# PSUM rings written out by hand, an earlier copy out of the attention bank, and a reordered start in a four-layer fp32 network

## The chip, the cores and the metric

The kernel runs on one core of one Trainium2 chip, all in fp32. The metric is the device time of one execution in microseconds (us), as the median of some runs. One further execution was profiled, and its own time differs a little from that median.

The core has five engines with their own instruction queues: TensorE (PE, with its weight loads, PEld), VectorE (DVE), ScalarE (ACT), GpSimd (POOL) and SyncE (SP), which here only issues DMAs. ScalarE's and GpSimd's queues issue DMAs too. Matmuls write into PSUM, which has eight banks of 128 partitions x 512 fp32 numbers; VectorE and ScalarE read it.

## The reference

The input is x with 4 images of 512 channels and 32 x 32 = 1024 tokens. Each layer adds its result to x after a group norm (32 groups of 16 channels):

```python
x = x + L0(gn(x))   # attention with mixed heads
x = x + L1(gn(x))   # gate per channel
x = x + L2(gn(x))   # plain attention
x = x + L3(gn(x))   # memory of 2048 rows, best 8 per token
```

- Layer 0: q, k and v are 512 x 512 projections, in 8 heads of 64. The scores of the heads are mixed by an 8 x 8 matrix, put through a softmax over the keys, and normalized over the whole map of each head (instance norm, with gamma and beta). They then weigh v; a projection with a bias follows.
- Layer 1: the mean of each channel goes through a small circuit of rotations, whose angles are q_params, and through a linear map with a sigmoid. This gives one factor for each channel.
- Layer 2: softmax attention in 8 heads with projections of q, k, v and of the result.
- Layer 3: each token is multiplied with 2048 memory rows; the softmax of the 8 largest products weighs these 8 rows.

## The kernel before, in words

**Tiling.** B = 4 images, KC = 4 blocks of 128 channels, T = 1024 tokens, TC = 8 blocks of 128 tokens, NB = 512 columns. The layers are not run one after the other over all images: layer 0 goes through the four images; what belongs to layer 1 and the preparation of the next image are pieces laid between its steps; then layers 2 and 3 follow. Most instructions carry `pin`, which keeps them in program order on their engine, so the order of the code is the order of the queues. Instructions without it are placed by a scheduler.

**PSUM in layer 0.** Three double banks (`pairs`, L52) and two single ones, `pv_bank` (L53) and `pt_bank` (L54), are allocated once. Projections take `pairs[at % 3]` by an index given by the caller (`place`, L176). Small results go to `pt_bank`.

**The start.** Nine small parameters are loaded by ScalarE's queue (L64 to L82), among them b_proj, while SyncE's queue loads x's four blocks of channels and w_q, block by block (`first`, L299 to L303). GpSimd makes an identity (L87) and the averaging matrix of the groups, `gavg` (L93). For each block k, `stats(k)` (L308) takes statistics on VectorE, `means(k)` averages them over each group with a matmul, and has the deviations formed by three small GpSimd operations (L150 to L152). `deviations(k)` averages again and takes a power on GpSimd (L119), `normalize(k)` scales the block on VectorE (L326). `multiply(k, m)` adds block k's share to the q projection (L332). The order is written out at L338 to L354. Then `circuit` (L772) prepares layer 1's tables: it reads w_head in 32 tiny loads (L781), and its chain of VectorE operations is ahead of the evacuation of k (L414).

**A step of layer 0.** An image has STEPS = 32 steps of 32 queries. Each computes scores (L467), copies them out (ScalarE, L473), brings them into another layout by 8 DMAs, which SyncE and GpSimd issue (L482), mixes heads (L493), takes exps (ScalarE, L500), turns them (VectorE, L506) and gathers statistics (L521). Seven steps behind (LAG = 7), `apply` (L523) weighs v with them and adds up in `pv_bank`, over four steps for each tile j. `take_out(b, j)` (L590) then has ScalarE copy `pv_bank` into a tile with the tag o1, which GpSimd scales (L605). Seven further steps, 32 to 38, end the image (L1559). In steps 32 to 35 the next image's q projections run as `piece` (L1510), one in each, into `pairs[(s + 1) % 3]`, and `put_q` (L291) has ScalarE copy q out. In `step` (L1436) `take_out` comes after `piece`: in step 34, tile j = 6 is copied behind that step's q. After the last image q belongs to layer 2 and is evacuated by VectorE (L1145).

**From layer 0 to layer 2.** Behind the last image come k (indices m + 1, L1569), v (i + 2, L1586) and the output projection `put_out` (m, L1588; evacuated on VectorE at L684, statistics at L699). Then the PSUM pool is closed and two new pools are opened: `ps_s` with three double banks and `ps_m` with two single ones (L1590 to L1595). In layers 2 and 3 each product takes a new tile from these pools.

**Layers 2 and 3.** `scores2` (L1165) computes four score tiles of a unit (L1183); ScalarE takes their exps (L1177). `apply2` (L1206) weighs v with the unit before (L1220). `invert2` (L1240) takes another tile for the sums of the softmax (`rs`, L1251). `seven` (L1033) computes a projection from seven products of half-size blocks; in `seven_k` ScalarE copies the first of them out four times (L1073). `attention` (L1326) multiplies with the memory, `read` and `read_last` (L1400, L1387) put together and transpose the result.

Of the kernel before, what the change touches and what calls it, by code (L numbers as in the profile page):

```python
# [10 lines left out]
F32 = mybir.dt.float32  # L11
# [30 lines left out]
def fast_net(ctx: ExitStack, tc: tile.TileContext, a: dict, out: bass.AP, flag: bass.AP):  # L42
# [18 lines left out]
        return pt_bank  # L61


    def chan(src, name):  # L64
        t = const.tile([P, KC], F32, tag=name, name=name)
        nc.scalar.dma_start(out=t, in_=src)
        return t

    gamma = const.tile([P, NH], F32, tag="gamma", name="gamma")
    nc.scalar.dma_start(out=gamma, in_=a["in_gamma"].partition_broadcast(P))  # L70
    beta = const.tile([P, NH], F32, tag="beta", name="beta")
    nc.scalar.dma_start(out=beta, in_=a["in_beta"].partition_broadcast(P))
    bproj = chan(a["b_proj"], "bproj")
    bq2 = chan(a["bq"], "bq2")
    bk2 = chan(a["bk"], "bk2")
    bp2 = chan(a["bp"], "bp2")
    fcb = chan(a["fc_b"], "fcb")

    fcw = const.tile([NQ, C], F32, tag="fcw", name="fcw")
    nc.scalar.dma_start(out=fcw, in_=a["fc_w"])  # L80
    qpar = const.tile([P, NL * NQ], F32, tag="qpar", name="qpar")
    nc.scalar.dma_start(out=qpar, in_=a["q_params"].partition_broadcast(P))  # L82

    whp = const.tile([P, NH], F32, tag="whp", name="whp")

    ident = const.tile([P, P], F32, tag="ident", name="ident")
    make_identity(nc, ident)  # L87
    ones = const.tile([P, P], F32, tag="ones", name="ones")
    nc.gpsimd.memset(ones, 1.0)
    mhalf = const.tile([P, NH], F32, tag="mhalf", name="mhalf")  # L90
    nc.gpsimd.memset(mhalf, -0.5)

# [8 lines left out]
        out=gavg_v, in_=gavg_v, compare_op=ALU.is_ge, fill=0.0, base=GSZ - 1,  # L101
        pattern=[[GSZ, P // GSZ], [0, GSZ]], channel_multiplier=-1,
    )
    NS = 32


# [68 lines left out]

    def place(at, name):  # L176

        return pairs[at % 3] if at is not None else ps_s.tile([P, 2, NB], F32, tag="sc", name=name)

    def flat2(ps):  # L180
        return ps.rearrange("p n q -> p (n q)")
# [112 lines left out]
    def first():  # L294

        I = img[0]
        xn = I["xn"] = xn_all
        w = I["w_q"] = eight_k([P, KC, C], "w_q0_0", 0)
        for k in range(KC):  # L299
            nc.sync.dma_start(out=xn[:, k, :], in_=x_v[0, :, k, :])  # L300
            nc.sync.dma_start(out=w[:, k, :], in_=a["w_q"][:, k, :])
        I["w_k"] = load_w("w_k", "w_k0_0", 1)
        I["w_v"] = load_w("w_v", "w_v0_0", 2)  # L303
        q = I["q"] = big("q", "q0_0")
        ybar = I["ybar"] = small.tile([P, KC], F32, tag="ybar", name="ybar0")
        parts, found = {}, {}

        def stats(k):  # L308
            mv = small.tile([P, 2], F32, tag="mv0", name=f"mv0_{k}")
            st = small.tile([P, 2, 6], F32, tag="bnst", name=f"st_a0_{k}")  # L310
            for i in range(2):
                pin(nc.vector.bn_stats(st[:, i, :], xn[:, k, i * NB:(i + 1) * NB]))
            pin(nc.vector.bn_aggr(mv, st.rearrange("p i s -> p (i s)")))
            parts[k] = group_coeffs_parts(mv[:, 0:1], mv[:, 1:2], f"a0_{k}")

        def means(k):
            next(parts[k])
            next(parts[k])

        def deviations(k):  # L320
            next(parts[k])
            found[k] = next(parts[k])

        def normalize(k):
            gm, rstd, dm = found[k]
            pin(nc.vector.tensor_scalar(  # L326
                xn[:, k, :], xn[:, k, :], gm, rstd, ALU.subtract, ALU.mult))
            pin(nc.gpsimd.tensor_mul(ybar[:, k:k + 1], dm, rstd))

        def multiply(k, m):  # L330
            for n in range(T // NB):
                pin(nc.tensor.matmul(  # L332
                    pairs[m][:, n, :],
                    w[:, k, m * P:(m + 1) * P], xn[:, k, n * NB:(n + 1) * NB],
                    start=(k == 0), stop=(k == KC - 1),
                ))
# [696 lines left out]
    def seven(b, key, src, multiply, view, block, begin, done=None):  # L1033

        a11, s2, s5, a22 = quarters(img[b][key], H)
        s1, s6, s7 = places7[key]
        b11, t6, t7, b22 = quarters(src, NB)
        t1, t3, t4 = places7["in"]
        factors = {1: (s1, t1), 2: (s2, b11), 3: (a11, t3), 4: (a22, t4),
                   5: (s5, b22), 6: (s6, t6), 7: (s7, t7)}  # L1040
        for i, (at, uses) in enumerate(SEVEN):
            ps = ps_s.tile([P, 2, NB], F32, tag="sc", name=f"{key}_{b}_{at}")
# [122 lines left out]
    def scores2(b, u, before=None):  # L1165
# [12 lines left out]
            es.append(e)  # L1178

        for i, t in enumerate(range(t0, t0 + 4)):  # L1180
            sc = ps_s.tile([P, 2, NB], F32, tag="sc", name=f"sc_{nm}_{t}")
            for r in range(2):
                pin(nc.tensor.matmul(  # L1183
                    sc[:, r, :],
                    I["k"][r * HD:(r + 1) * HD, m, t * P:(t + 1) * P],
                    I["q"][r * HD:(r + 1) * HD, m, n * NB:(n + 1) * NB],
                    start=True, stop=True,
                ))
            scs.append(sc)
            if before is None or i < 2:  # L1190
                exp2()
# [14 lines left out]
    def apply2(b, u, exp2=None):  # L1206
# [33 lines left out]
    def invert2(b):  # L1240
# [4 lines left out]
            return  # L1245
        m, n = I["ready"] = due
        nm = f"{b}_{m}_{n}"
        ps = ps_s.tile([P, 2, NB], F32, tag="sc", name=f"rs_{nm}")[:, 0, 0:NS]
# [77 lines left out]
    def attention(b, tt, between=None):  # L1326
# [2 lines left out]
        att = eight_k([P, NI], f"att_{nm}")  # L1329
        for i, (lo, hi) in enumerate(  # L1330
                ((0, T), (T, T + NB), (T + NB, NI)) if (b, tt) == tiles[-1] else ((0, T), (T, NI))):
            sc = ps_s.tile([P, T], F32, tag="sc", name=f"at_{nm}_{i}")
# [54 lines left out]
    def read_last(b, tt, picked, dg):  # L1387

        got, et, rs, xr = picked
        tp = ps_m.tile([P, KC, P], F32, tag="mm", name=f"stp_{b}_{tt}")  # L1390
        for i in range(TOPK):
            for m in range(KC):
                pin(nc.tensor.matmul(
# [6 lines left out]
    def read(b, tt, picked):  # L1400
# [9 lines left out]
        tp = ps_m.tile([P, KC, P], F32, tag="mm", name=f"stp_{nm}")  # L1410
# [25 lines left out]
    def step(b, s, mid, piece):  # L1436
# [103 lines left out]
    for b in range(B):  # L1540
# [38 lines left out]
        if last:  # L1579
# [13 lines left out]
    stage = ctx.enter_context(ExitStack())  # L1593
    ps_s = stage.enter_context(tc.tile_pool(name="ps_s2", bufs=3, space=PSUM))
    ps_m = stage.enter_context(tc.tile_pool(name="ps_m2", bufs=2, space=PSUM))  # L1595

    def small_ps(name):
        return ps_s.tile([P, 2 * NB], F32, tag="sc", name=name)
# [81 lines left out]
    def check_range():  # L1680

        tot = small.tile([P, 1], F32, tag="tot", name="tot")
        nc.vector.tensor_reduce(tot, seen0, AX.X, ALU.add)
        tps = ps_m.tile([P, NB], F32, tag="mm", name="tot")
# [748 lines left out]
```

## Time and profile before

| | before |
|---|---|
| median of 3 runs | 2556.93 us (2554.43 to 2558.5) |
| the profiled execution, its own time | 2558.39 us |
| span from its first to its last instruction | 2556.6 us |
| mean granted clock of TensorE | 0.998 |
| layer 0, four images with layer 1 between | about 0 to 1267 us of the span |
| layer 2 | about 1267 to 2090 us |
| layer 3 | to the end |
| matmuls in the span | 18534 instructions |

The profile gives the busy time of each engine and its share of the span. It lists what ended each idle time of an engine, as "waited for", and shows timelines of single engines. Each row of a timeline holds the start, the length, the engine, the line of the code, the operation, and the tile written from the tile read; equal neighbours are merged (x16). In brackets is the idle time ahead of it with what ended it. The fp32 matmuls of the program are two instructions each in the trace, each with its own weight load.

### The profile page before, as it was taken

What the parts mean: (1) busy time and instruction counts of PE and PEld (TensorE: products, weight loads), DVE (VectorE), ACT (ScalarE), POOL (GpSimd) and SP (SyncE); (2) the same over time, 40 slices, a digit from 0 to 9 for tenths busy, and PEclk for the clock granted to TensorE, in tenths of its full rate; (3) what the DMA queues carried; (4) which work ended last, traced back from release to release, by engine and by line L of the source; (5) the groups of instructions that cost most, each with busy time, mean ns of one, the idle gap of its engine ahead of it and who ended that gap; (6) DMA issues with size and microseconds to landing.
All of it is one profiled execution on the core that took longest, in us unless ns stands there. A gap on an engine that the chain in (4) does not pass through costs nothing.

```text
span 2556.6 us, 47828 instructions
## 1 busy us (share of the span) xinstructions
PE 2503.3 (98%) x18534; PEld 1180.8 (46%) x18534; DVE 1685.8 (66%) x2785; ACT 985.8 (39%) x1177; POOL 1192.5 (47%) x1700
## 2 busy tenths in 40 slices
PE   8999999999999999999999999999999999999998
PEld 3344534554355534555633533453353344444445
DVE  4599448872688438881267567576657648788875
ACT  1467336651666336651153145125314612121211
POOL 3266415553465425553074147117405617566655
PEclk9999999999999999999999999999999999999999
DMA  2578438872698428982301130121014046767665
GB/s 83 145 207 237 125 120 226 244 211 74 172 243 235 131 82 211 244 248 101 124 16 55 70 112 18 54 83 59 21 54 148 18 130 190 219 186 217 187 184 170
DMA packets 187211, 361.39 MB, mean 141 GB/s; under 512 B 32729, under 2 KB 96217, under 8 KB 182882
## 3 DMA queue, kind: packets, MB, share of 16 engines
q1 hardware_dynamic: 105744, 178.71, 22.6%
q0 software_dynamic: 49152, 142.79, 20.6%
q10 hardware_dynamic: 32082, 36.76, 5.3%
q8 instruction: 149, 2.44, 0.4%
q14 instruction: 84, 0.69, 0.1%
HBM read 186.96 MB, written 36.96 MB: 88 GB/s over the span
## 4 chain that ended last, share of the span: by engine, by line
PE 74%; issue 10%; POOL 7%; DVE 3%; ACT 3%; DMA 2%; POOLq 0%; SPq 0%; ACTq 0%; DVEq 0%
PE pair L192 10%; PE sc_c L1183 9%; PE pv_c L1220 9%; PE pv L532 8%; POOL got L1360 7%; PE pair L467 6%; PE pair L493 5%; PE pt L425 5%; PE pt L721 4%; PE q L192 3%; PE Wk L1056 3%; PE Wv L1063 3%; ACT e L500 2%; PE Wp L1056 2%; PE at L1335 2%
## 5 line engine op out<-in xcount | busy, mean ns | idle before, releaser
L482 POOL DMA_DIRECT2D s<-ss x512 | 258.2, 511 | 399.5 <-PE pair L493 113.4
L506 DVE STREAM_TRANSPOSE eT<-e 128x1024 f32<-128x1024 f32 x256 | 316.5, 1236 | 193.6 <-ACT e L500 193.0
L1360 POOL DMA_INDIRECT got<-in_mem,ix x256 | 279.5, 1092 | 213.2 <-issue 122.1
L1177 ACT ACTIVATE eT<-sc_c 128x1024 f32<-128x1024 f32 x256 | 248.0, 1022 | 330.7 <-PE sc_c L1183 204.8
L521 DVE BATCH_NORM_STATS2 st<-e 128x6 f32<-128x256 f32 x1024 | 350.7, 404 | 0.0
L500 ACT ACTIVATE e<-pair 128x1024 f32<-128x1024 f32 x256 | 250.7, 1022 | 167.5 <-PE pair L493 137.2
L1201 POOL TENSOR_TENSOR e<-eT 128x1024 f32<-128x1024 f32 x96 | 232.3, 2421 | 168.6 <-DVE out L1125 69.5
L467 PE MATMUL pair<-k,q 64*32 64x512 f32 x4096 | 267.4, 598 | 12.7 <-ACT e L500 12.7
L473 ACT COPY ss<-pair 128x1024 f32<-128x1024 f32 x256 | 247.3, 1020 | 77.5 <-DMA s<-ss 37.9
L532 PE MATMUL pv<-eT,v 128*64 128x128 f32 x4096 | 250.7, 276 | 8.9 <-ACT pv L592 8.9
L532 PEld LDWEIGHTS pv<-eT,v 128*64 128x64 f32 x4096 | 221.1, 137 | 76.7 <-issue 54.5
L1183 PE MATMUL sc_c<-q,k 64*128 64x512 f32 x1024 | 240.9, 607 | 3.1 <-DVE xr L684 2.3
L1220 PE MATMUL pv_c<-eT,v 128*64 128x512 f32 x1024 | 233.0, 597 | 0.0
L1202 DVE TENSOR_TENSOR eT<-eT,e 128x1024 f32<-128x1024 f32 x96 | 136.3, 1420 | 146.3 <-POOL e L1201 146.1
L1197 POOL TENSOR_TENSOR eT<-eT 128x1024 f32<-128x1024 f32 x32 | 77.8, 2433 | 206.8 <-ACT eT L1177 202.8
L1407 DVE SCALAR_TENSOR_TENSOR acc<-got,et,acc 128x512 f32<-128x512 f32 x210 | 157.9, 752 | 7.5
L493 PE MATMUL pair<-s,wmix 32*32 32x512 f32 x4096 | 160.6, 600 | 2.3 <-issue 2.1
L1183 PEld LDWEIGHTS sc_c<-q,k 64*128 64x128 f32 x1024 | 93.6, 187 | 141.0 <-issue 71.9
L1340 ACT COPY att<-at 128x1024 f32<-128x1024 f32 (+1 forms) x65 | 64.9, 999 | 219.7 <-PE at L1335 212.9
L467 PEld LDWEIGHTS pair<-k,q 64*32 64x32 f32 x4096 | 57.0, 105 | 179.9 <-ACT e L500 86.2
L1220 PEld LDWEIGHTS pv_c<-eT,v 128*64 128x64 f32 x1024 | 68.0, 137 | 136.8 <-issue 136.8
L1335 PE MATMUL at<-memT,xn_d 128*128 128x512 f32 x256 | 120.7, 594 | 0.0
(335 smaller groups left out, 3431.3 us busy)
## 6 DMA issues: line engine op xcount, KB each, us to landing
s<-ss SPq DMA_DIRECT2D x512, 128.0 KB
s<-ss POOLq DMA_DIRECT2D x512, 128.0 KB
rb<-r POOLq DMA_DIRECT2D x64, 128.0 KB
o<-o SPq DMA_DIRECT2D x32, 256.0 KB
xr<-in_x ACTq DMA_DIRECT2D x32, 256.0 KB
x<-xr SPq DMA_DIRECT2D x32, 256.0 KB
xr_c<-x SPq DMA_DIRECT2D x32, 256.0 KB
rb_c<-r SPq DMA_DIRECT2D x64, 128.0 KB
```

The lines of the kernel that those rows point to most:

```text
L192: pin(nc.tensor.matmul(ps[:, n, :], w[:, k, m * P:(m + 1) * P], rhs(k, n), start=(k == 0), stop=(k == KC - 1),))
L467: pin(nc.tensor.matmul(sc[m * NS:(m + 1) * NS, r, :], q[r * HD:(r + 1) * HD, m, s * NS:(s + 1) * NS], k_[r * HD:(r + 1) * HD, m, n * NB:(n ...
L482: pin(relays[side].dma_start(out=s2[2 * m + r::NH], in_=ss[m * NS:(m + 1) * NS, r, :]))
L493: pin(nc.tensor.matmul(mixed(s, r // 2)[t * NS:(t + 1) * NS, r % 2, :].rearrange("p (qq k) -> p qq k", qq=2), wmix[r * NS:(r + 1) * NS], s ...
L500: pin(nc.scalar.activation(e[:, half].rearrange("p r qq k -> p (r qq k)"), flat2(mixed(s, half)), AF.Exp))
L506: pin(nc.vector.transpose(eT[:, j % 2].rearrange("p b (qq i r) x -> p i r qq b x", qq=2, i=4)[:, i, 2 * half:2 * half + 2], e[:, half].rea ...
L521: pin(nc.vector.bn_stats(st[:, i, 2 * half + r, qq, :], e[:, half, r, qq, :]))
L532: pin(nc.tensor.matmul(pv[r * HD:(r + 1) * HD, gp, :], I["v"][:, t, g * HD:(g + 1) * HD], eT[:, j % 2, t, :, 4 * g:4 * g + 4], start=(t == ...
L1177: pin(nc.scalar.activation(e, scs[len(es)], AF.Exp))
L1183: pin(nc.tensor.matmul(sc[:, r, :], I["k"][r * HD:(r + 1) * HD, m, t * P:(t + 1) * P], I["q"][r * HD:(r + 1) * HD, m, n * NB:(n + 1) * NB] ...
L1220: pin(nc.tensor.matmul(pv[r * HD:(r + 1) * HD, :], I["v"][:, t, h * HD:(h + 1) * HD], e[:, r, :], start=(t == 0), stop=(t == TC - 1),))
L1360: pin(nc.gpsimd.indirect_dma_start(out=got[:, i, :], out_offset=None, in_=a["mem"], in_offset=bass.IndirectOffsetOnAxis(ap=ix[:, i:i + 1], ...
```

## The change

1. The nine parameters are loaded by the same queue, ScalarE's, but the lines stand behind SyncE's loads of x and w_q in the program (`later`). The identity is made after `gavg`; the matrix of ones is made first and pinned.
2. x's first block of channels is loaded in two halves. Statistics are taken half by half, the second block's second half after `deviations(0)`, and `normalize(0)` comes ahead of `means(1)`. The deviations are formed on VectorE by three operations. 17 matmuls of `ones` with itself are laid in TensorE's queue ahead of and between these (`warm`).
3. In steps 32 and later, `take_out` comes directly after `apply`, ahead of the q projection.
4. The two new pools go. Layers 2 and 3 take `pairs` in turn (`next_pair`) and `pt_bank` and `pv_bank` in turn (`next_bank`). The indices of k, v and the output projection of the last image are shifted so that the output projection takes pairs 2, 0, 1, 2 and layer 2 begins with pair 0.

```diff
-    nc.scalar.dma_start(out=gamma, in_=a["in_gamma"].partition_broadcast(P))
...
+    later = []
+
+    def held(shape, name, src):
+        t = const.tile(shape, F32, tag=name, name=name)
+        later.append(lambda: nc.scalar.dma_start(out=t, in_=src))
+        return t
...
+        for n in range(2):
+            nc.sync.dma_start(out=xn[:, 0, n * NB:(n + 1) * NB], in_=x_v[0, :, 0, n * NB:(n + 1) * NB])
         for k in range(KC):
-            nc.sync.dma_start(out=xn[:, k, :], in_=x_v[0, :, k, :])
+            if k > 0:
+                nc.sync.dma_start(out=xn[:, k, :], in_=x_v[0, :, k, :])
             nc.sync.dma_start(out=w[:, k, :], in_=a["w_q"][:, k, :])
+        for load in later:
+            load()
...
         def means(k):
...
+            pin(nc.tensor.matmul(ps[:, 0:1], gavg, mv[:, 0:1], start=True, stop=True))
+            dm, sq, gm = (column(name, k) for name in ("dm", "gsq", "gm"))
+            pin(nc.vector.tensor_sub(dm, mv[:, 0:1], ps[:, 0:1]))
+            pin(nc.vector.scalar_tensor_tensor(sq, dm, dm, mv[:, 1:2], ALU.mult, ALU.add))
+            pin(nc.vector.tensor_copy(gm, ps[:, 0:1]))
...
+        def warm(times):
+            for _ in range(times):
+                pin(nc.tensor.matmul(pairs[2][:, 0, 0:P], ones, ones, start=True, stop=True))
...
-        stats(0)
+        warm(11)
+        for i in range(2):
+            stats(0, i)
         means(0)
-        stats(1)
+        stats(1, 0)
+        warm(2)
         deviations(0)
+        stats(1, 1)
+        warm(2)
+        normalize(0)
         means(1)
-        normalize(0)
+        warm(2)
         for k in range(KC):
             if k + 2 < KC:
-                stats(k + 2)
+                for i in range(2):
+                    stats(k + 2, i)
...
             apply(b, s - LAG)
+        if s >= STEPS and tiled and part == 3:
+            take_out(b, j)
         if not tiled or s >= STEPS:
             piece(b, s)
...
-        if tiled and part == 3:
+        if tiled and part == 3 and s < STEPS:
             take_out(b, j)
...
-            ks[m](m + 1)
+            ks[m](m + 1 + last)
...
-                take_v2(0, i, i + 2)
+                take_v2(0, i, i + 1)
             for m in range(KC):
-                put_out(b, m, m)
-
-    stage.close()
-    pairs.clear()
+                put_out(b, m, m + 2)
...
-    ps_s = stage.enter_context(tc.tile_pool(name="ps_s2", bufs=3, space=PSUM))
-    ps_m = stage.enter_context(tc.tile_pool(name="ps_m2", bufs=2, space=PSUM))
+    turns = [0, 0]
+
+    def next_pair():
+        turns[0] += 1
+        return pairs[(turns[0] - 1) % 3]
+
+    def next_bank():
+        turns[1] += 1
+        return (pv_bank, pt_bank)[turns[1] % 2]
...
-            sc = ps_s.tile([P, 2, NB], F32, tag="sc", name=f"sc_{nm}_{t}")
+            sc = next_pair()
...
-            I["pv", m, n] = ps_m.tile([P, NB], F32, tag="mm", name=f"pv_c{b}_{m}_{n}")
+            I["pv", m, n] = next_bank()
```

Every other tile of `ps_s` and `ps_m` is replaced in the same way.

More of the change, by code (lines that the diff above doesn't have):

```diff
@@ L61, in small_ps @@
         return pt_bank
-    def chan(src, name):
-        t = const.tile([P, KC], F32, tag=name, name=name)
-        nc.scalar.dma_start(out=t, in_=src)
-        return t
-    gamma = const.tile([P, NH], F32, tag="gamma", name="gamma")
-    nc.scalar.dma_start(out=gamma, in_=a["in_gamma"].partition_broadcast(P))
[L71 to L82, printed above, removed]
+    later = []
+    def held(shape, name, src):
+        t = const.tile(shape, F32, tag=name, name=name)
+        later.append(lambda: nc.scalar.dma_start(out=t, in_=src))
+        return t
+    gamma = held([P, NH], "gamma", a["in_gamma"].partition_broadcast(P))
+    beta = held([P, NH], "beta", a["in_beta"].partition_broadcast(P))
+    bproj = held([P, KC], "bproj", a["b_proj"])
+    bq2 = held([P, KC], "bq2", a["bq"])
+    bk2 = held([P, KC], "bk2", a["bk"])
+    bp2 = held([P, KC], "bp2", a["bp"])
+    fcb = held([P, KC], "fcb", a["fc_b"])
+    fcw = held([NQ, C], "fcw", a["fc_w"])
+    qpar = held([P, NL * NQ], "qpar", a["q_params"].partition_broadcast(P))
     whp = const.tile([P, NH], F32, tag="whp", name="whp")
-    ident = const.tile([P, P], F32, tag="ident", name="ident")
-    make_identity(nc, ident)
     ones = const.tile([P, P], F32, tag="ones", name="ones")
-    nc.gpsimd.memset(ones, 1.0)
+    pin(nc.gpsimd.memset(ones, 1.0))
     mhalf = const.tile([P, NH], F32, tag="mhalf", name="mhalf")
@@ L103, in fast_net @@
     )
+    ident = const.tile([P, P], F32, tag="ident", name="ident")
+    make_identity(nc, ident)
     NS = 32
@@ L176, in place @@
     def place(at, name):
-        return pairs[at % 3] if at is not None else ps_s.tile([P, 2, NB], F32, tag="sc", name=name)
+        return pairs[at % 3] if at is not None else next_pair()
     def flat2(ps):
@@ L306, in first, with stats, column @@
         parts, found = {}, {}
[L308 to L314, printed above, removed]
-        def means(k):
-            next(parts[k])
-            next(parts[k])
-        def deviations(k):
-            next(parts[k])
-            found[k] = next(parts[k])
+        def stats(k, i):
+            if i == 0:
+                parts[k] = (
+                    small.tile([P, 2], F32, tag="mv0", name=f"mv0_{k}"),
+                    small.tile([P, 2, 6], F32, tag="bnst", name=f"st_a0_{k}"))
+            mv, st = parts[k]
+            pin(nc.vector.bn_stats(st[:, i, :], xn[:, k, i * NB:(i + 1) * NB]))
+            if i == 1:
+                pin(nc.vector.bn_aggr(mv, st.rearrange("p i s -> p (i s)")))
+        def column(name, k):
+            return small.tile([P, 1], F32, tag=f"{name}1", bufs=2, name=f"{name}_a0_{k}")
+        def means(k):
+            mv = parts[k][0]
+            ps = small_ps(f"gps_a0_{k}")
+            pin(nc.tensor.matmul(ps[:, 0:1], gavg, mv[:, 0:1], start=True, stop=True))
[3 more added lines that the diff above has]
+            pin(nc.vector.tensor_copy(gm, ps[:, 0:1]))
+            found[k] = gm, dm, sq
+        def deviations(k):
+            gm, dm, sq = found[k]
+            ps = small_ps(f"gps2_a0_{k}")
+            pin(nc.tensor.matmul(ps[:, 0:1], gavg, sq, start=True, stop=True))
+            ve, rstd = column("gve", k), column("grstd", k)
+            pin(nc.vector.tensor_scalar_add(ve, ps[:, 0:1], GN_EPS))
+            pin(rsqrt(rstd, ve))
+            found[k] = gm, rstd, dm
+        def warm(times):
+            for _ in range(times):
+                pin(nc.tensor.matmul(pairs[2][:, 0, 0:P], ones, ones, start=True, stop=True))
         def normalize(k):
@@ L1041, in seven @@
         for i, (at, uses) in enumerate(SEVEN):
-            ps = ps_s.tile([P, 2, NB], F32, tag="sc", name=f"{key}_{b}_{at}")
+            ps = next_pair()
             multiply(ps, *factors[at])
@@ L1247, in invert2 @@
         nm = f"{b}_{m}_{n}"
-        ps = ps_s.tile([P, 2, NB], F32, tag="sc", name=f"rs_{nm}")[:, 0, 0:NS]
+        ps = next_pair()[:, 0, 0:NS]
         s_ = I.pop(("s", m, n)).rearrange("p r q -> p (r q)")
@@ L1331, in attention @@
                 ((0, T), (T, T + NB), (T + NB, NI)) if (b, tt) == tiles[-1] else ((0, T), (T, NI))):
-            sc = ps_s.tile([P, T], F32, tag="sc", name=f"at_{nm}_{i}")
+            sc = flat2(next_pair())
             for i0 in range(lo, hi, NB):
@@ L1389, in read_last @@
         got, et, rs, xr = picked
-        tp = ps_m.tile([P, KC, P], F32, tag="mm", name=f"stp_{b}_{tt}")
+        tp = next_bank().rearrange("p (k q) -> p k q", q=P)
         for i in range(TOPK):
@@ L1409, in read @@
             ))
-        tp = ps_m.tile([P, KC, P], F32, tag="mm", name=f"stp_{nm}")
+        tp = next_bank().rearrange("p (k q) -> p k q", q=P)
         for m in range(KC):
@@ L1585, in fast_net @@
             for i in range(TC // 2):
-                take_v2(0, i, i + 2)
+                take_v2(0, i, i + 1)
             for m in range(KC):
-                put_out(b, m, m)
-    stage.close()
-    pairs.clear()
+                put_out(b, m, m + 2)
     by_scalar.append(True)
-    stage = ctx.enter_context(ExitStack())
-    ps_s = stage.enter_context(tc.tile_pool(name="ps_s2", bufs=3, space=PSUM))
-    ps_m = stage.enter_context(tc.tile_pool(name="ps_m2", bufs=2, space=PSUM))
+    turns = [0, 0]
[5 more added lines that the diff above has]
+        return (pv_bank, pt_bank)[turns[1] % 2]
     def small_ps(name):
-        return ps_s.tile([P, 2 * NB], F32, tag="sc", name=name)
+        return flat2(next_pair())
     places2 = eT_flat[:, 0:6 * 2 * NB].rearrange("p (i r q) -> p i r q", i=6, r=2)
@@ L1683, in check_range @@
         nc.vector.tensor_reduce(tot, seen0, AX.X, ALU.add)
-        tps = ps_m.tile([P, NB], F32, tag="mm", name="tot")
+        tps = next_bank()
         nc.tensor.matmul(tps[:, 0:1], ones, tot, start=True, stop=True)
```

## The prediction

> **What bounds the kernel now.** I read the page first, then who TensorE waited for, then the timelines around those waits. The page:
>
> ```profile
> PE 2503.3 (98%) x18534; PEld 1180.8 (46%) x18534; DVE 1685.8 (66%) x2785; ACT 985.8 (39%) x1177; POOL 1192.5 (47%) x1700
> ```
>
> TensorE is busy for 2503.3 of 2556.6 us. No other engine passes 66%. A change that takes no matmul away can win only in the 53.3 us in which TensorE stands still, or where a busy matmul runs slowly. The waits of TensorE's matmuls (total us, times, longest) show where it stands still:
>
> ```profile
> PE pair L467 <- ACT e L500: 12.7, 57, 1.5
> PE pv L532 <- ACT pv L592: 8.9, 15, 1.6
> PE pt L145 <- DVE mv L313: 7.3, 1, 7.3
> ...
> PE sc_c L1183 <- DVE xr L684: 2.3, 1, 2.3
> ...
> PE Wk L1056 <- ACT k L1073: 2.0, 1, 2.0
> ```
>
> The first row, inside layer 0's steps, is not touched. The other four are. The timeline behind an image's steps (start, length, engine, line; the wait ahead of it in brackets) shows the second row:
>
> ```profile
> 287.83 7.13 PE L192 MATMUL pair<-xn_all,w_q 128*128 128x512 f32 x16
> 296.55 1.97 PE L532 MATMUL pv<-eT,v 128*64 128x128 f32 x32 [1.59 <-ACT pv L592]
> ...
> 295.00 1.01 ACT L292 COPY q<-pair 128x1024 f32<-128x1024 f32 x1 [6.86 <-PE pair L192]
> 295.91 0.59 ACT L592 COPY pv<-pv 128x512 f32<-128x512 f32 x1
> ```
>
> The tile in pv_bank was complete before 287.9. ScalarE sat idle for 6.86 us, but its queue held the q copy ahead of the pv copy, so pv came out only once the projection and both copies were done. TensorE paid 1.59 us. The same place costs 1.47 in each of the next two images; in the last, q leaves by VectorE and there is no wait.
>
> From layer 1's end to layer 2:
>
> ```profile
> 1267.48 8.83 PE L1183 MATMUL sc_c<-q,k 64*128 64x512 f32 x32 [2.32 <-DVE xr L684]
> ...
> 1268.25 0.40 PEld L1183 LDWEIGHTS sc_c<-q,k 64*128 64x128 f32 x2 [0.45 <-issue]
> 1269.10 0.40 PEld L1183 LDWEIGHTS sc_c<-q,k 64*128 64x128 f32 x2 [0.45 <-issue]
> ...
> 1271.83 0.22 PEld L1183 LDWEIGHTS sc_c<-q,k 64*128 64x128 f32 x2 [0.21 <-issue]
> 1272.26 0.22 PEld L1183 LDWEIGHTS sc_c<-q,k 64*128 64x128 f32 x2 [0.21 <-ACT eT L1177]
> ```
>
> The first score tile waits 2.32 us for the last evacuation of layer 0, though two of the three pairs had been read out long before. And then the weight loads come 0.85 us apart up to about 1271.4, and 0.43 apart after it: for 3.9 us TensorE ran at half rate. The page's row of granted clock does not show that; the spacing does.
>
> The start:
>
> ```profile
> 1.73 0.43 SPq L300 DMA_DIRECT2D xn_all<-in_x  x1
> 8.14 1.29 DVE L312 BATCH_NORM_STATS2 st_a<-xn_all 128x6 f32<-128x512 f32 x2
> 8.32 0.33 SPq L301 DMA_DIRECT2D w_q<-in_w_q  x1
> 11.31 3.78 PE L332 MATMUL pair<-xn_all,w_q 128*128 128x512 f32 x4 [0.97 <-DVE xn_all L326]
> 15.10 1.96 PE L332 MATMUL pair<-xn_all,w_q 128*128 128x512 f32 x4
> ```
>
> Four matmuls take 3.78 us at 11.31 and 1.96 at 15.10: half rate again. Between 11 and 70 us TensorE is busy for 58.69 of 59, so what is won here stays won. SP issues nothing from 2.2 to 8.32; its wait is put down to the parameter DMA of b_proj.
>
> **What the Trainium skill says.** "TensorE: Matmul & The Clock Gate", What's actually happening: an idle array falls to half its clock and is released after about 3.4 us of activity. The trace agrees: 3.8 and 3.9 us at half rate. "PSUM — Partial Sum Buffer", PSUM bank collisions: accesses by two engines are to be kept apart bank by bank; so a ring needs only its own banks' readers to be done, which the 2.32 us wait goes beyond. "DMA: Bandwidth & Descriptors", Queues, rings and completion order: each DMA engine takes turns between queues at packet granularity; so small parameter packets can hold up x. The trace fits it: parameters issued at 1.74 landed near 8.1.
>
> **The change, part by part.**
>
> *Copy of pv ahead of the q projection.* Same instructions, other order on ScalarE. It concerns steps 34 and 38; at 38 no projection follows. At 34 the 0.59 us copy goes into the 6.86 us idle; the q copy behind it still waits for its projection. The tile o1 that it writes was last read by GpSimd before 272.5. Removed: 1.59 + 1.47 + 1.47 = **4.5 us**; bounds 4.3 and 4.7. Late next: nothing shown, pv's keys were turned by 291.
>
> *The boundary.* The new rotation ends layer 0 on pair 2 (put_out takes 2, 0, 1, 2), and layer 2 starts with pair 0, last read when m=1 left at about 1255.1. So the first scores start at 1265.2. Pair 2 comes third, a warm 0.91 us per tile later, at 1267.0; its last bank is free at 1267.35, a wait of 0.35 that hides behind the exps. With no gap the clock stays up. First score ready 1266.1, exps from 1266.2 at 0.945 each (five in 4.72); tile 8 needs the fifth exp: 1266.2 + 4.7 = 1270.9, and ends at 1271.85. Before it ended at 1276.32. Gain **4.4 us**; if the clock falls all the same, 1.9.
>
> *Wk's wait.* In program order q3, Wk1, rs, gps_b, Wk4 over three places: the ring gives Wk4 the place of Wk1, as before, so its four copies of 0.6 us still count. Tracked by bank, the first bank is free one copy earlier: **0.6 us**, from 0 to 2.0. Elsewhere in layers 2 and 3 TensorE waits for no place, and a ring of three in the order of the matmuls does what a pool of three did: 0.
>
> *The start.* TensorE gets 17 warm-up matmuls, two instructions each, in a time in which it has nothing to do before 7.28. The 128-column transposes of layer 3 run at 0.43 us per four instructions; the first 22 take 2.4 us at full rate, 4.7 at half, so 1.1 to at most 5.8. The mean is ready at about 5.9 to 6.2 (it was 7.13; the second half of x's channels lands no later than the whole did, 5.6, and only 0.68 of statistics remains). If they overran by 1 us, x's second channels, needed next, would still cover it. These landed at 8.12. The bytes ahead are the same; without parameter packets I take 7.4, bounds 7.0 and 8.1. From there: statistics 0.7, add 0.15, second half and aggregate 0.95 (they hide GpSimd's 0.58 power), normalize 0.85, hand-over 0.1: first product at 7.4 + 2.75 = 10.15, 1.15 earlier. At full clock 1.95 is saved on the first four matmuls. Together 3.1. Then x's third channels: the way from their landing to the next product is 13.78 to 17.04 = 3.3 us, and they are needed by about 10.6; before, they landed at 13.76, since SP had been held. With SP free the data between (0.79 MB at the 315 GB/s of the slices from 5 to 7 us) takes 2.5 us after 7.4: 9.9. Tight, so I take **2.5 us**. Bounds 4.5 and -2: that parameters (nine DMAs, now on ScalarE's queue with nothing ahead of it) still hold one of SP's loads. GpSimd's identity, moved behind gavg, is first used at 24. VectorE's three small operations replace GpSimd's: they lie before x lands. The 32 loads of w_head end at 37.6; they move with SP's queue, and VectorE's chain behind them held the first k copy until 56.4, harmless while the third bank is wanted later; 3 us less of TensorE leaves that so.
>
> Sum: 4.5 + 4.4 + 0.6 + 2.5 = 12.0 us. The profiled execution took 2558.4 (span 2556.6, 1.8 around it): 2546.4. The median of the runs is 1.5 below it: **2544.9**, say 2545.
>
> **Rivals.** (1) The parameters still hold SP: no gain at the start or a loss of 2. For it: ScalarE's queue has nothing ahead of them. Against: they come after the loads in program order. 2547.4 to 2549.4. (2) The start fails and the boundary keeps half of its cost: 4.5 + 1.9 - 2 = 4.4, so 2552.5. (3) Slower: the rings of layer 2. A unit's fourth score tile takes the first one's pair; its exp ends at 1282.05 and the tile starts at 1282.6, a slack of 0.57. A rotation shifted by the small tiles, or an exp that comes later by more than this, makes TensorE wait in all 64 units; at 0.3 us each that is 19 us, against 12: 2564. It decides from 0.19 us a unit. Against it: the order is that of the pool, and before no unit waited.
>
> **Chances.** Forecast 0.62, (1) 0.18, (2) 0.12, (3) 0.08. A measurement can tell about 0.2%, 5.1 us, from no change. Faster: the first two, 0.80; same: 0.12; slower 0.08. Range: gains from 15.5 (4.7 + 4.5 + 2.0 + 4.3) down to 4.4: 2541.4 to 2552.5.
>
> **What would show it.** The wait of pv for its copy falls from 8.9 to about 4.4. No wait and no 0.85 us spacing of loads after layer 0. The first products near 10, four in 1.9. Wk's wait at 1.4. Wrong it would be if score tiles wait for exps in each unit, or SP stops again within the first loads.

## The result: slower by 0.3%, and the profile after

The changed kernel takes 2564.75 us (median of 8 runs, 2560.31 to 2568.41) against 2555.64 for the kernel before (8 runs): a ratio of 1.003, with an interval from 1.0019 to 1.0041. Faster by 12 us was forecast. The profiled execution took 2565.16 us, its span is 2563.4.

The lines of the code that count here have moved by 22 to 29: the scores are L1212 now (L1183 before), the weighing with the exps L1249 (L1220), the half-size products L1085 and L1092 (L1056, L1063), their additions on VectorE L1022 (L993), the first products L354 (L332). All double banks are called pair now, the single ones pt and pv. Wk, Wv and Wp stand for layer 2's projections that `seven` computes, for k, v and the result.

The page's first part shows that TensorE got more to do, not less:

```profile
PE 2516.0 (98%) x18568; PEld 1186.7 (46%) x18568; DVE 1675.6 (65%) x2793; ACT 985.6 (38%) x1177; POOL 1188.5 (46%) x1688
```

The 34 instructions that were added are warm-ups; they account for 6.6 of the 12.7 us by which TensorE is busier. The other 6 are matmuls that took longer. The waits of TensorE (total us, times, longest):

```profile
PE pair L1212 <- DVE out L1022: 10.3, 3, 3.7
PE pv L561 <- ACT pv L621: 4.3, 12, 1.0
...
PE pair L1085 <- ACT k L1102: 2.0, 1, 2.0
...
PE pair L1212 <- DVE xr L713: 0.3, 1, 0.3
```

The rows of pv and of xr are as forecast: the wait for the copy of pv fell from 8.9 to 4.3, the one at the boundary from 2.3 to 0.3. The first row is new. Three times score tiles wait for VectorE, 10.3 us in all.

To see where time came and went, I take the same events in both traces:

| event | before | after | after minus before |
|---|---|---|---|
| last 12 of the first products begin | 22.86 | 22.48 | -0.38 |
| first scores of layer 2 can begin (before: at the start of the wait) | 1265.16 | 1260.14 | -5.02 |
| first weighing in layer 2 begins | 1276.25 | 1267.79 | -8.46 |
| second of the Wk products begins | 1419.80 | 1411.36 | -8.44 |
| first of the Wv products begins | 1441.31 | 1434.45 | -6.86 |
| layer 3's first product behind the last output projection of layer 2 | 2089.68 | 2100.67 | +10.99 |
| end | 2556.6 | 2563.4 | +6.8 |

Up to the start of layer 2 the change won 8.5 of the 12 us. Between the first Wv products and layer 3, 17.8 us were lost, in a stretch to which the prediction had given a change of 0. In layer 3, 4.2 us came back, of which the last section speaks.

**Where the 17.8 us were lost.** The three waits all stand behind `seven_out`, which computes the output projection of layer 2 (Wp). This is the timeline of the kernel before at the second of these places (start, length, engine, line, operation; idle ahead of it and its releaser in brackets):

```profile
1710.96 3.60 PE L1056 MATMUL Wp<-eT 128*128 128x512 f32 x8
...
1714.48 4.70 PE L1183 MATMUL sc_c<-q,k 64*128 64x512 f32 x16
...
1716.80 0.30 PEld L1183 LDWEIGHTS sc_c<-q,k 64*128 64x128 f32 x4 [0.76 <-ACT eT L1177]
...
1718.95 1.17 DVE L993 TENSOR_TENSOR out<-out,Wp 128x1024 f32<-128x1024 f32 x1
1719.11 3.65 PE L1220 MATMUL pv_c<-eT,v 128*64 128x512 f32 x16
```

and this the same place after:

```profile
1713.37 2.38 PE L1212 MATMUL pair<-q,k 64*128 64x512 f32 x8
...
1718.24 1.17 DVE L1022 TENSOR_TENSOR out<-out,pair 128x1024 f32<-128x1024 f32 x1
1719.46 0.51 PEld L1212 LDWEIGHTS pair<-q,k 64*128 64x128 f32 x4 [4.54 <-DVE out L1022]
1719.46 3.79 PE L1212 MATMUL pair<-q,k 64*128 64x512 f32 x8 [3.72 <-DVE out L1022]
...
1720.48 0.34 PEld L1212 LDWEIGHTS pair<-q,k 64*128 64x128 f32 x2 [0.51 <-issue]
1721.33 0.34 PEld L1212 LDWEIGHTS pair<-q,k 64*128 64x128 f32 x2 [0.51 <-issue]
```

The last of the seven Wp tiles is added by VectorE late, because bias, residual and statistics of other blocks stand ahead of it: it is done at 1720.1 before and at 1719.4 after. Before, all four score tiles of the unit were computed from 1714.48 to 1719.1 without the pair of the last Wp tile: the weight load of the third, at 1716.80, waits for ScalarE's exp of the first score tile, whose pair it takes. The pool gave out the pair that came free first. After, the ring goes on in order: the third score tile takes the pair of the last Wp tile, although the first score tile's exp is done at 1715.6. TensorE waits 3.72 us; and the loads behind come 0.85 us apart, so the next tiles run at half rate. For the same thing at the first of the three places, the view of stretches gives a granted clock of 0.50 for 1494.19 to 1498.00. Eight score matmuls take 3.79 us, where they take 1.99 at full rate (experiment 3), and the weighing behind them (from 1723.18) 4.63 instead of 3.65. From the first Wp product to the scores of the next unit, the three places lost 5.7, 6.2 and 5.9 us: 17.8.

### The profile page after: what moved, and what is told of

Same layout as the page of the kernel before. It is cut to its first block, busy times and chain, and to the rows that moved or that the text cites. A ratio compares the mean times of both kernels' runs of the same rounds, so it can differ in the third digit from the quotient of the medians.

```text
span 2563.4 us, 47864 instructions
## 1 busy us (share of the span) xinstructions
PE 2516.0 (98%) x18568; PEld 1186.7 (46%) x18568; DVE 1675.6 (65%) x2793; ACT 985.6 (38%) x1177; POOL 1188.5 (46%) x1688
## 4 chain that ended last, share of the span: by engine, by line
PE 74%; issue 8%; POOL 7%; DMA 6%; DVE 2%; ACT 2%; SPq 0%; POOLq 0%; ACTq 0%; DVEq 0%
PE pair L189 15%; PE pair L1212 9%; PE pv L561 8%; POOL got L1389 7%; PE pair L496 6%; PE pair L522 5%; PE pair L1085 5%; PE pt L1249 5%; PE pt L454 5%; PE pv L1249 4%; PE pt L750 4%; DMA got<-in_mem,ix 3%; PE pair L1092 3%; DMA s<-ss 2%; ACT e L529 2%
## 5 line engine op out<-in xcount | busy, mean ns | idle before, releaser
L1206 ACT ACTIVATE eT<-pair 128x1024 f32<-128x1024 f32 x256 | 248.2, 1022 | 344.8 <-PE pair L1212 210.5
L1212 PE MATMUL pair<-q,k 64*128 64x512 f32 x1024 | 244.3, 615 | 11.0 <-DVE out L1022 10.3
L1231 DVE TENSOR_TENSOR eT<-eT,e 128x1024 f32<-128x1024 f32 x96 | 127.9, 1332 | 169.0 <-POOL e L1230 168.8
L1212 PEld LDWEIGHTS pair<-q,k 64*128 64x128 f32 x1024 | 94.2, 189 | 149.4 <-issue 70.5
L1369 ACT COPY att<-pair 128x1024 f32<-128x1024 f32 (+1 forms) x65 | 64.9, 999 | 220.9 <-PE pair L1364 220.7
L1364 PE MATMUL pair<-memT,xn_d 128*128 128x512 f32 x256 | 120.7, 594 | 0.0
L1364 PE MATMUL pair<-memT,eT 128*128 128x512 f32 x256 | 120.4, 593 | 0.0
L1364 PE MATMUL pair<-eT 128*128 128x512 f32 x256 | 120.3, 592 | 0.0
```

Of the source, the lines that this page charges most:

```text
L1206: pin(nc.scalar.activation(e, scs[len(es)], AF.Exp))
L1212: pin(nc.tensor.matmul(sc[:, r, :], I["k"][r * HD:(r + 1) * HD, m, t * P:(t + 1) * P], I["q"][r * HD:(r + 1) * HD, m, n * NB:(n + 1) * NB] ...
L1364: pin(nc.tensor.matmul(sc[:, i0 - lo:i0 - lo + NB], xn3[b][:, k, tt * P:(tt + 1) * P], memT[k][:, i0:i0 + NB], start=(k == 0), stop=(k == ...
```

## The experiments

The theory after the traces: the rings cost 17.8 us at three places since they take places in order, while the pool took them as they came free; about 60% of it is the wait, the rest the low clock. The rival: the wait is VectorE's lateness, or work per unit is slower in general, and another order of places doesn't help. A second question is why the start gave nothing.

Single runs of one kernel lie up to 10 us from their median, and the traces of the changed kernel and of experiments 1 to 3, whose code up to layer 2 is the same, reach layer 2 at 1260.14, 1260.02, 1264.37 and 1264.50 us. So times are told with intervals, what one place costs is measured at that place, and of the 5.02 us in the table's second row only the 4.6 by which the waits for pv fell can be told from scatter.

**1. Reuse the scores' pairs at all three places.** The ring hands out the pairs i, i + 1, i, i + 1 instead of i, i + 1, i + 2, i behind `seven_out`, so that no score waits for the last Wp tile:

```diff
+    def reuse_scores():
+        at = turns[0]
+        forced.extend((at, at + 1, at, at + 1))
+        turns[0] = at + 2
...
         seven_out(b)
+        reuse_scores()
```

> The changed kernel, but the first four score tiles behind each of layer 2's three Strassen-like output projections take pairs i, i+1, i, i+1 and not i, i+1, i+2, i: the third one reuses the first score tile's pair, as the pool let it. Ring theory (the third score tile waits for the pair of the last product, which VectorE reads last): the three waits of 3.3 to 3.7 us for VectorE's out go, and the half-rate stretch behind each; 3 x 6.0 = 18 us less than the changed kernel's 2564.8: about 2547. Rival (the loss is spread over layer 2's units, or comes from the order of unpinned work): 2560 or more.

2551.05 us, a ratio to before of 0.998 (0.9973 to 0.9986): 13.7 less than the changed kernel by the medians. The row of waits for L1022 is gone. The place shown above, in this kernel's timeline:

```profile
1707.61 4.68 PE L1212 MATMUL pair<-q,k 64*128 64x512 f32 x16
1712.21 3.65 PE L1249 MATMUL pt<-eT,v 128*64 128x512 f32 x16
```

Sixteen score matmuls in one piece of 4.68 us, as before (4.70), at full clock. From one place to the next it is 219.1 us, as before; in the changed kernel it is 225. Layer 3 begins 17.9 us earlier than in the changed kernel. Of the 17.9 us 13.4 are left at the end of the trace (2550.0 against 2563.4), since its layer 3 is 4.5 us longer, though nothing there was edited. The cause is shown at the three places; the time as a whole lies between the theory's forecast and the rival's.

**2. The same at one place only.** The call stands under `if b == 1`.

> As the first kernel, but only at the second of the three places. Ring theory: a third of the gain, 6 us less than 2564.8, 2559; in the profile the wait for VectorE's out is gone at the second place alone. Rival: no third of anything; 2564 or, if one place sets the others, all of it.

2559.2 us, 1.0015 (1.0008 to 1.0023). Two waits are left, of 6.6 us. One place less is worth 5.5 us by the medians, three 13.7, so within the scatter it adds up place by place.

**3. Keep the clock up over the wait.** The changed kernel, with twelve matmuls of `ones` into a free bank ahead of the third score tile:

```diff
+            if i == 2 and u == UNITS2[1] and b > 0:
+                for _ in range(12):
+                    pin(nc.tensor.matmul(
+                        (pv_bank, pt_bank)[turns[1] % 2][:, 0:P], ones, ones, start=True, stop=True))
```

> The changed kernel with 12 idle matmuls (24 instructions, 2.6 us at full rate) of the matrix of ones into a free single bank ahead of the third score tile at the three places: the wait stays, TensorE is busy in it. Clock theory (half of the loss is TensorE's clock, which falls in the wait): score pairs and the next weighing of v run at full rate; 3 x 2.9 = 8.7 us less: 2556. Rival (the slow stretch is ScalarE's exps, which come late): unchanged, 2564 to 2566.

2559.49 us, 1.0013 (1.0004 to 1.0023), so 5.3 less than the changed kernel. At the first and the third place the matmuls fill the wait but for 0.43 us, and what follows runs at full rate (3.65 for the weighing); these places are 2.75 and 2.98 us shorter. At the second, VectorE came later still: x's old value landed 8.8 us after its issue, the addition that reads it took 2.83 us where others take 0.75, and a wait of 3.3 us stayed. So of some 5.9 us at a place, about 2.9 are the low clock and 3 the wait itself. This is why a wait of 10.3 us in the list cost 17.8.

**4. The rings alone.** The kernel before with the rings and shifted indices, and nothing else of the change.

> The kernel before with the rings of layers 2 and 3 and the shifted indices alone: no earlier copy of pv, start as before. Ring theory: boundary of layers 0 and 2 -3.4, three places +18, Wk's stretch 0 to +1.6: 2570 to 2572, slower than the changed kernel. Rival (the rings are neutral, the loss comes with the shift in time of the other parts): 2552 to 2556.

2571.71 us, 1.0057 (1.0043 to 1.007), with the same three waits (9.9 us). By the ratio the rings alone make the kernel 14.6 us slower (11 to 18), in spite of the gain at the boundary.

**5. The early copy of pv alone.** The kernel before with `take_out` moved.

```diff
+        if s >= STEPS and tiled and part == 3:
+            take_out(b, j)
```

> The kernel before with one part of the change: in steps 32 and later the copy of pv goes ahead of the q projection's copy. Theory: this part is independent of the rings, so it gives what the trace of the changed kernel showed at the start of layer 2, about 4.6 us: 2550.8, and the wait of pv for its copy falls from 8.9 to about 4.3. Rival: in the changed kernel it only shifted the wait, and without the rings it gives less than 2 us: 2554 or above.

2551.64 us, 0.9985 (0.9975 to 0.9995), and the wait is at 4.3: 3.8 us won, with an interval that holds the 4.6 of the waits.

**6. The start alone.** The kernel before with points 1 and 2 of the change: the parameters moved, the halves of x, the deviations on VectorE and the warm-ups.

> The kernel before with the other part alone: the nine parameters behind the loads in the program, x's first channels in halves, 17 warm-up matmuls. Theory: parameters still hold SyncE's loads of x, so the last twelve first products begin within 0.5 us of before and the time is 2555.0 to 2555.6. Rival: this part was slowed by something else in the changed kernel, and gives its forecast 2.5 us alone: 2553.

2556.71 us, 1.0006 (0.9998 to 1.0014), with the last twelve of the first products at 23.36 (22.86 before). This part wins nothing.

In the changed kernel's start SyncE still stops:

```profile
1.73 0.43 SPq L301 DMA_DIRECT2D w_q<-in_w_q  x1
4.50 0.33 SPq L300 DMA_DIRECT2D xn_all<-in_x  x1
6.01 0.33 SPq L301 DMA_DIRECT2D w_q<-in_w_q  x1
...
8.74 0.69 DVE L316 BATCH_NORM_STATS2 st_a<-xn_all 128x6 f32<-128x512 f32 x1 [1.74 <-DMA xn_all<-in_x]
...
11.16 3.10 PE L354 MATMUL pair<-xn_all,w_q 128*128 128x512 f32 x4
...
22.48 5.57 PE L354 MATMUL pair<-xn_all,w_q 128*128 128x512 f32 x12
```

It issues x's second block at 4.50 instead of about 2.2. ScalarE's queue starts on the parameters at 0.80 (gamma), 1.26 (beta) and 1.74 (b_proj), since nothing is ahead of them there: standing behind the loads in the program doesn't put them behind the loads in time. And the first four products take 3.10 us, again at a low clock for the most part in spite of the warm-ups.

**7. The parameters really late.** Experiment 1, with the nine loads pinned in ScalarE's queue behind the copies of the first q tiles:

```diff
-        for load in later:
-            load()
...
         for m in range(2):
             put_q(q, m)(flat2(pairs[m]))
+        for load in later:
+            load()
```

> The kernel of the run in which the scores behind Wp reuse the pairs of the first two, with one thing more: the nine parameter loads stand in ScalarE's queue behind the copies of the first q tiles, so that they are issued only after about 25 us. Theory: they held SyncE's queue; now SyncE issues x and w_q without a stop from 0.8 us on, x's second channels land near 7.4 instead of 8.7 and the third near 10 instead of 12.6, and the start gains 2 to 3 us: 2548.5. Rival: x comes late by the width of the DMA, or VectorE's chain of statistics sets the first products: less than 0.7 us, 2550.4 or above.

2550.35 us, 0.9976 (0.9969 to 0.9984): 0.7 less than experiment 1, within the scatter. My theory fell. SyncE now issues all of x and w_q from 0.81 to 5.9 without a stop, so the parameters did hold it; but x's second block lands at 8.31, hardly earlier than with the stop (8.74 after, 8.14 before). Only the third comes earlier: its statistics start at 10.98, not at 12.61. The first four products take 3.62 us and the last twelve begin at 23.02. In experiment 1, with the same warm-ups, it was the other way round: four products in 1.89 at 10.67, then a wait for x's third block to 16.88, and the last twelve at 22.72. Two hindrances stood side by side, the clock and the third block: in each of these two traces one is gone and the other sets the time. Which of them comes is not set by the parameters alone; the last section returns to the clock.

**8. Another bank for the sums ahead of Wk's second product.** Experiment 7, with the sums of the softmax in the free single bank in the first half of Wk's products, so that the second product doesn't take the pair of the first:

```diff
-                invert2(b)
+                invert2(b, (pv_bank, pt_bank)[(turns[1] + 1) % 2])
```

> The same as the run with the late parameters, with one edit more: in the first half of Wk's products the sums of the softmax go into the free single bank instead of a pair, so that Wk's second product doesn't take the pair that ScalarE still copies out four times. Theory: the wait of 2.0 us and the stretch at half rate behind it (8.7 instead of 7.1 us) both go: 3.5 us less than the run with the late parameters, 2545. Rival: the wait stays, since the next product has to wait for the same copies: no difference.

2545.79 us, 0.9959 (0.9944 to 0.9974). The changed kernel's second Wk product, in its timeline:

```profile
1411.36 8.71 PE L1085 MATMUL pair<-sums,Wk 128*128 128x512 f32 x16 [1.96 <-ACT k L1102]
```

and this kernel's, with the next:

```profile
1412.01 7.11 PE L1085 MATMUL pair<-sums,Wk 128*128 128x512 f32 x16
1419.83 7.13 PE L1085 MATMUL pair<-xn_c,Wk 128*128 128x512 f32 x16 [0.59 <-ACT k L1102]
```

From the first Wk product to the first Wv product it takes 26.35 us instead of the 29.43 of experiment 7: 3.1 won, 0.6 of the wait having moved to the third product. 3.5 were expected.

**9. Warm-ups through the gap.** Experiment 8, with eight instead of two warm-ups behind the deviations of x's first block and none ahead of the products:

```diff
         deviations(0)
         stats(1, 1)
-        warm(2)
+        warm(8)
         normalize(0)
         means(1)
-        warm(2)
```

> The run with late parameters and the other bank for Wk, with the warm-up matmuls laid differently: eight instead of two behind the deviations of x's first channels, none behind the means of the second. Theory: with the parameters out of the way the start was still cold, since TensorE stood 1.6 to 2.0 us before those means; with that gap filled the first four products take 1.9 instead of 3.62 us and begin no later, the last twelve begin near 20.5 instead of 22.7 us, and 2 us are won: 2543.8. Rival: x's second and third channels come late by then, so a wait of VectorE's normalize takes the place of the slow products: less than 0.7 us, 2545.1 or above.

The start in this trace:

```profile
7.15 2.03 PE L342 MATMUL pair<-ones 128*128 128x128 f32 x16
...
10.76 1.98 PE L352 MATMUL pair<-xn_all,w_q 128*128 128x512 f32 x4 [0.29 <-DVE dm_a L326]
...
12.72 1.96 PE L352 MATMUL pair<-xn_all,w_q 128*128 128x512 f32 x4
```

Behind the first warm-up there is no idle time above 0.9 us, the first product already runs at full clock, and the last twelve begin at 20.48, as expected (20.5) and 2.2 us earlier than in experiment 8. The lead is still there 70 us later: the same score matmuls begin at 90.84 us here and at 93.04 in experiment 8. The time, 2546.13 us, 0.9964 (0.9951 to 0.9976), can't tell 2 us from none: steps of layer 0 differ by as much from trace to trace. The gain at the start is shown in the trace; that it arrives at the end is not.

**10. No warm-ups at all.**

> The same as the run before it, without any warm-up matmul. Theory: the first products begin some 0.5 us earlier than with two warm-ups ahead of them but run at half rate for about 3.5 us, so the last twelve begin at 22.0 to 22.7 us: 2545.2 to 2545.8, as in the run with the other bank for Wk. Rival: warm-ups are worth nothing either way, and it equals the run with the gap filled.

2547.17 us, 0.9964 (0.9954 to 0.9975). The first four products take 3.78 us and the last twelve begin at 23.72, a us later than expected, because x's second block landed at 8.84 in this run. Counted from that landing, the way to the last twelve is 14.9 us here, 14.7 before, 13.7 in the changed kernel, 14.5, 15.3, 14.7 and 15.1 in experiments 1, 6, 7 and 8, and 12.1 in experiment 9. So warm-ups with a gap behind them are worth a us at the best and nothing on average, and with the gap filled some 2.7 us.

The best of these, experiments 8 to 10, are 0.36 to 0.41% faster than the kernel before, and not told apart by their times.

## Why the prediction was wrong, point by point

**The step that failed** is in the paragraph on Wk's wait: "Elsewhere in layers 2 and 3 TensorE waits for no place, and a ring of three in the order of the matmuls does what a pool of three did: 0." The first half was nearly true of the kernel before: the list has no such wait of a matmul, but the sixteen score matmuls behind Wp took 4.70 us where other units' took 3.70, and the third tile's weight load waited for an exp: even the pool was short of places there. The second half doesn't follow from it. At this place the pool gave out the pair whose reader was done first; a ring gives the next one. They are the same only where tiles are released in the order in which they are made. Behind `seven_out` the last Wp tile, read by a busy VectorE, is released after two younger score tiles, read by an idle ScalarE. The price was 17.8 us in the trace, where the prediction had 0; experiments 1, 2 and 4 show that the order is the cause. The profile of before held the evidence: at that place the third score's weight load waited for an exp and not for VectorE, while the Wp tile made before the scores was read only 2 us later. I had looked at TensorE's waits, and there was none of any size there to be seen.

**Early copy of pv**: right. Forecast 4.5, the wait fell by 4.6, and alone it gave 3.8 (1.3 to 6.4).

**The boundary**: right in its mechanism, 3.4 in place of 4.4. The first scores begin at once, and no low clock follows:

```profile
1260.14 1.99 PE L1212 MATMUL pair<-q,k 64*128 64x512 f32 x8
1262.44 5.42 PE L1212 MATMUL pair<-q,k 64*128 64x512 f32 x24 [0.31 <-DVE xr L713]
1267.79 3.65 PE L1249 MATMUL pt<-eT,v 128*64 128x512 f32 x16
```

But from the first score to the first weighing it takes 7.65 us, not 6.65. The 0.31 us wait of the third tile was not hidden: it held ScalarE's exps by 0.36. And the estimate was too short even without it: in experiment 5, where the scores once started meet no wait, it takes 7.07. There the same wait of 2.32 us stands ahead of the first score, and yet the 32 score matmuls take 7.14 us where they took 8.83 before. So the half rate didn't belong to the wait as such; against experiment 5 the boundary gains 1.7 us and not 3.4.

**Wk's wait**: wrong by 2.2. Forecast was a gain of 0.6, since I took it that a product waits for its own bank alone; the wait stayed at 1.96. Then 1.6 us were lost, for the product behind ran at half rate (8.71, where it was 7.13 before). Experiment 6, in which there are no rings, has 8.83 as well, so the rings are not its cause.

**The start**: forecast 2.5, and 0.4 came in the trace, nothing in experiment 6. Rival (1) named the mechanism: parameters still held SyncE. Its counterargument, "they come after the loads in program order", was what failed. But even this was half of it: experiment 7 took the hold away and won nothing, since x's second block lands no earlier for it, and the clock was the other hindrance. "TensorE: Matmul & The Clock Gate", What's actually happening, in the Trainium skill, names about 3.4 us of activity until full clock; the traces agree, in which the stretches at half clock behind a wait last 3.41 us or twice that. My error was to count how long TensorE works and not what idle time follows. A sum was a little off too: four products in 1.96 and not 3.78 us save 1.8, not 1.95.

**Rival (3)** was the only one on the right side, and by luck near in size (2564). Its place and mechanism were wrong: not 64 units of 0.3 us waiting for exps, but three places of 5.9 us waiting for VectorE. Its argument against itself, "the order is that of the pool", was the failed step again.

The sum in the traces' numbers: 0.4 (start) + 4.6 (the copy) + 3.4 (boundary) - 1.6 (Wk) - 17.8 (three places) + 4.2 (layer 3, not credited to the change) = -6.8.

## What to carry to other kernels

Before a pool of buffers is written out as a ring, look in the trace for a place where an older tile is released after a younger one: there the pool reorders and the ring waits, and "no wait now" is no proof that the order doesn't matter. A wait of TensorE of some 3 us costs the low clock behind it too, here about as much again (3 + 2.9 us). And to warm a clock up, fill the last gap before the work; what was done before that gap counted for little here.

## What had not been expected

- **A gap of about 2 us lowers the clock in some runs and not in others.** Ahead of Wk's second product TensorE stands for 1.96 us in the kernel before and in eight others here. The product behind took 7.13 us in two of these nine (before, experiment 5) and 8.7 to 8.8 in the other seven. At the boundary, 2.3 to 2.5 us of wait gave half rate before and in experiment 6, none in experiment 5. At the start, gaps of 1.6 and 2.0 us gave half rate (experiments 8 and 7), one of 1.9 didn't (experiment 1), one of 0.9 didn't (experiment 9). Behind the waits of 3.3 to 3.7 us at the three places a stretch at half rate followed in every trace. The traces show what most of it hangs on: where the gap falls. From the first record on, the granted clock is 1 or 0.50 and changes only at the borders of pieces of 3.41 us, which lie elsewhere in each trace. Before, TensorE stands still for 2.3 us of the piece from 1264.31 to 1267.72, and the next piece has 0.50. In experiment 5 a border at 1262.53 cuts the same wait into 1.3 and 1.0 us, and no low piece follows. Over all twelve traces, up to the last matmul, there are 31 pieces at full clock in which TensorE stands still for 1.7 us or more, half a piece; 29 are followed by a low one. Of some 85 pieces with 0.8 to 1.7 us, 8 are, and of the others none. Ahead of Wk's second product 1.77 of the 1.96 us lie in one piece in the changed kernel, 1.47 in experiment 5; the kernel before is one of the two exceptions, with 1.89 us in one piece and full clock behind it. This is read from the traces; no run shifted a gap against the border.
- **The row of slices hides it, the view of stretches doesn't.** The page's row of granted clock is at 9 throughout in both kernels. Taken over 4 us alone, the granted clock is 0.50 (after, 1494.19 to 1498.00) and 0.57 (before, 1267.5 to 1271.5).
- **Layer 3 has two lengths.** From its first product behind the last output projection to the end it takes 465.7 to 467.2 us before and in experiments 1, 5, 7 and 8, but 462.5 to 463.1 after and in the other six, with the same work. In each of the five long traces TensorE stands still for 1.7 to 2.3 us of one piece of 3.41 around the start of its last 32 matmuls, which read gathered memory rows, and the piece behind it, in which they run, is at half clock; in none of the seven short ones is it so. And from the last matmul to the end it takes 5.3 to 6.8 us in the long traces, 4.8 to 4.9 in the short ones. It goes neither with the rings (experiments 1 and 2 both have them) nor with the warm-ups. Why TensorE stands longer there and the last write takes longer in some traces stays open, and the 4.2 us that the changed kernel gained there are not credited to the change.
